# Layer 0 router on four token tiles at once in 32-column parts of TensorE, and an attention end written out without steps

## The chip, the cores and the metric

The kernel runs on one core of one Trainium2 chip. The metric is the device time of one execution, in microseconds (us). Three executions of the kernel before took 3007.15, 3005.03 and 3000.24 us; the median is 3005.03 us. A profiled execution, taken by the hardware profiler, is shown beside them.

Names of engines in the profile: PE is TensorE (PEld its weight loads), DVE is VectorE, ACT is ScalarE, POOL is GpSimd, SP is SyncE, which here only issues DMAs.

## The reference, cut to what matters

Two layers are computed on x, which has 2 x 2048 tokens of 512 numbers (4096 tokens, 32 tiles of 128). Each layer is a cross attention over 154 context rows and a feed-forward part with 8 experts. The change touches only the end of the first attention and the scores by which tokens are given to experts:

```
x = x + xattn(layernorm(x), ctx, w_q, w_k, w_v, w_o)      # 16 heads of 32
xf = layernorm(x).reshape(-1, 512)
scores = softmax(xf @ router_w + router_b, axis=-1)       # 8 experts
G, idx = top_k(scores.T, 1024)                            # each expert picks 1024 tokens
toks = xf[idx]                                            # gathered rows
...
```

All of it is float32.

## The kernel before, in words

**Tiles and steps.** A tile is 128 tokens (`NT` = 32 tiles), a block is four tiles (`TPB` = 4, `NB` = 8 blocks). The first attention runs as a software pipeline: `step(G)` is called for G = 0 to 37 (`for G in range(LAST + 10)`, with `LAST` = 28). One step works on many tiles at once, each at another stage: the scores and exponentials of block-and-head-group G (`scores_of`, `exp_of`, four tiles each), the transposed probabilities of G - 1 (`probs_t`), the product with the values of G - 2 (`values`), the output projection of tile G - 5 (`project`), its residual (`residual`, tile G - 6), the normalised row of tile G - 10 (`norm_x1`, on GpSimd), its transpose (`transpose_x1`, tile G - 11) and the router product of the same tile (`router`). Every fourth step ends with `logits` and `router_scores` of one block.

**What sets the order.** In this stage PE, DVE, ACT and POOL run exactly in the order in which the lines are written; only the order of the DMAs on SP's queue is chosen by the framework's scheduler. An instruction that waits holds up all that stands behind it on its engine.

**Two buffers matter.** The scores live in one PSUM tile `sc` with one buffer, so `scores_of(G, 3)` cannot start on PE before `exp_of(G, 2)` has read the tile of `scores_of(G, 2)`; between the two stand DVE's minimum (L289) and subtraction (L290) and ACT's two exponentials (L301). Nearly all else that PE writes (`ps_q`, `pt`, `pp`, `ps_l`, `ps_o`, `pl`) shares three PSUM buffers with the tag `gen`.

**The router before.** `router(u)` multiplies the router's weights, 128 rows of 8 columns, four times (`KC` = 4 parts of the 512 features) with one transposed tile of 128 tokens. A float32 product takes two passes, so it is 8 instructions on PE (L376). ACT copies the 8 x 128 result to `lT` (L377). When four tiles are there, `logits` turns them back with four small transposes (L384) and DVE and ACT make the softmax; `router_scores` writes the scores into the last 8 columns of each normalised row and sends the row to DRAM (`xs`, L403), 260 KB a tile.

**The end before.** After the loop come the last tiles' norms, transposes and routers. What follows is the choice of 1024 tokens per expert: a search over 30 bits in which DVE and PE take turns (L591 to L595). Its buffers (`sco`, `iota_i`, `same` and others) lie where rows and other tiles of the attention lay, so POOL's first instruction there (L533) and DVE's copy of the scores (L574) wait for the last row store to have landed.

Of the kernel before, what the change touches and what calls it, by code (L numbers as in the profile page):

```python
# [10 lines left out]
F32 = mybir.dt.float32  # L11
# [4 lines left out]
ALU = mybir.AluOpType  # L16
# [18 lines left out]
E = 8  # L35
# [20 lines left out]
def two_layers(ctx: ExitStack, tc: tile.TileContext, a, out):  # L56
# [51 lines left out]
    def transpose_tile(src, dstT, t, psum, tag, bufs=2):  # L108

        pt = psum.tile([P, KC, P], F32, tag=tag, name="pt", bufs=bufs)  # L110
        for k in range(KC):
            nc.tensor.transpose(pt[:, k, :], src[:, ts(k, P)], ident)  # L112
        nc.scalar.copy(dstT[:, :, ts(t, P)], pt)  # L113
# [9 lines left out]
    with (  # L123
# [4 lines left out]
    ):  # L128
        wq = wa.tile([P, KC, D], F32, name="wq")
        wo = wa.tile([P, KC, D], F32, name="wo")  # L130
        rw = wa.tile([P, KC, E], F32, name="rw")
        kT = wa.tile([P, B, KC, TKV], F32, name="kT")
        vblk = wa.tile([P, B, KC, 4, 2, HD], F32, name="vblk")
        scale = HD**-0.5
# [23 lines left out]
        def roots(m):  # L158
            mv, rstd = roots_of(m)
            j = slice(0 if 0 <= m - 2 < NB else 1, 2 if m + 3 < NB else 1)  # L160
            nc.scalar.activation(rstd[:, j], mv[:, j, :, 1], AF.Sqrt, bias=eps_t)
            nc.vector.reciprocal(rstd[:, j], rstd[:, j])
# [29 lines left out]
        with tc.tile_pool(name="wk", bufs=1) as wkv:  # L192
            ctxT = wkv.tile([P, KC, B * TKV], F32, name="ctxT")
            nc.sync.dma_start(ctxT, a["ctxT"].rearrange("(k p) n -> p k n", p=P))
            wk = wkv.tile([P, KC, D], F32, name="wk")
            wv = wkv.tile([P, KC, D], F32, name="wv")
            for w, n in ((wk, "w_kT"), (wv, "w_vT"), (wq, "w_qT"), (wo, "w_oT"), (rw, "router_w")):
                nc.sync.dma_start(w, a[n].rearrange("(k p) n -> p k n", p=P))

            for v in range(TPB):  # L200
                stats(xt[v], -3, 1, v)
            roots(-3)
            for v in range(TPB):
# [28 lines left out]
            for b in range(B):  # L232
                cper = wkv.tile([P, KC, 4, TKV], F32, tag="cper", name="cper")
                for hh in range(4):
                    nc.gpsimd.tensor_copy(cper[:, :, hh, :], ctxT[:, :, ts(b, TKV)])
                for i in range(GC):
                    n = P if i < GC - 1 else GL
                    heads = sorted({i * P // TKV, (i * P + n - 1) // TKV})
                    h0, nh = heads[0], len(heads)
                    ps = pa.tile([P, KC, nh * HD], F32, tag="gen", name="ps_v", bufs=3)  # L240
                    for k in range(KC):
                        nc.tensor.matmul(
                            ps[:n],
                            cper[:, k].rearrange("p h n -> p (h n)")[:, i * P : i * P + n],
                            wv[:, k, :].rearrange("p (c d) -> p c d", c=KC)[:, :, h0 * HD : (h0 + nh) * HD],
                            start=k == 0,
                            stop=k == KC - 1,
                        )
                    for j in range(nh):
                        nc.vector.tensor_scalar_mul(  # L250
                            vblk[:n, b, :, h0 + j, i - h0 - j, :],
                            ps[:n, :, j * HD : (j + 1) * HD],
                            mask[:n, i, h0 + j : h0 + j + 1],
                        )
                    if b == 0 and i > 0:
                        transpose_x(TPB + i - 1)
                    if b == 0 and i < TPB:
                        norm_x(TPB + i)
                        load_x(2 * TPB + i)
                        ps_q = queries(0, i)  # L260
                        nc.scalar.copy(qT[0][:, i, :], ps_q)
                    if b == 1 and i < TPB:
                        stats(xt[2 * TPB + i], -1, 1, i)
            roots(-1)
            for i in range(TPB):
                load_x(3 * TPB + i)
                if i < TPB - 1:
                    stats(xt[3 * TPB + i], 0, 1, i)
            norm_x(2 * TPB)

        with tc.tile_pool(name="sa", bufs=2) as sa:
            prob, pTs, oT, x1t, row, x1T, lT, pend = {}, {}, {}, {}, {}, {}, {}, {}

            def tile_of(u):
                return 0 <= u < NT
# [84 lines left out]

            def norm_x1(u, eng=nc.vector):
                blk, i = divmod(u, TPB)
                row[u] = sa.tile([P, ROW], F32, tag="row", name="row", bufs=8)
                norm(row[u][:, 0:D], x1t.pop(u), blk + 2, 0, i, eng)

            def transpose_x1(u):
                x1T[u] = sa.tile([P, KC, P], F32, tag="x1T", name="x1T", bufs=4)
                transpose_tile(row[u][:, 0:D], x1T[u], 0, pa, "gen", 3)

            def router(u):  # L370
                blk, i = divmod(u, TPB)
                if i == 0:
                    lT[blk] = sa.tile([E, TPB, P], F32, tag="lT", name="lT")
                ps = pa.tile([E, P], F32, tag="gen", name="ps_l", bufs=3)
                for k in range(KC):
                    nc.tensor.matmul(ps, rw[:, k, :], x1T[u][:, k, :], start=k == 0, stop=k == KC - 1)  # L376
                nc.scalar.copy(lT[blk][:, i, :], ps)  # L377

            SL = [P, TPB, E]

            def logits(blk):
                pl = pa.tile(SL, F32, tag="gen", name="pl", bufs=3)
                for t in range(TPB):
                    nc.tensor.transpose(pl[:, t, :], lT[blk][:, t, :], ident[0:E, 0:E])  # L384
                lg = sa.tile(SL, F32, tag="lg", name="lg")
                lm = sa.tile([P, TPB, 1], F32, tag="lm", name="lm")
                nc.vector.tensor_tensor(lg, pl, rb_bc.unsqueeze(1).to_broadcast(SL), ALU.add)
                nc.vector.tensor_reduce(lm, lg, AX.X, ALU.max)
                nc.vector.tensor_tensor(lg, lg, lm.to_broadcast(SL), ALU.subtract)
                nc.scalar.activation(lg, lg, AF.Exp)  # L390
                lT[blk] = (lg, lm)

            def router_scores(blk):
# [6 lines left out]
                for t in range(TPB):  # L400
                    u = blk * TPB + t
                    nc.vector.tensor_copy(row[u][:, D:ROW], scores[:, :, u])
                    nc.sync.dma_start(xs[u * P : (u + 1) * P, :], row.pop(u))  # L403

            LAST = NT - TPB

            def step(G):
                m, i4 = divmod(G, TPB)
# [14 lines left out]
                    residual(G - 6, pend.pop("o"))  # L423
                if tile_of(G + TPB):
                    pend["q"] = queries(m + 1, i4)
                if tile_of(G - 11) and G - 11 < LAST:
                    transpose_x1(G - 11)
                if tile_of(G + 9):
                    norm_x(G + 9, nc.gpsimd)
# [22 lines left out]
                    probs_t(G - 1, 3)  # L452
                if tile_of(G + 8):
                    transpose_x(G + 8)
                if tile_of(G - 10) and G - 10 < LAST:
                    norm_x1(G - 10, nc.gpsimd)
                if tile_of(G - 11) and G - 11 < LAST:
                    router(G - 11)
                if on:
                    scores_of(G, 3)  # L460
                if before:
# [9 lines left out]
                    logits((G - 15) // TPB)  # L471
                    router_scores((G - 15) // TPB)

            for G in range(LAST + 10):
                step(G)
            roots(NB + 1)
            transpose_x1(LAST - 1)
            router(LAST - 1)
            for u in range(LAST, NT):
                norm_x1(u)  # L480
                transpose_x1(u)
            logits(NB - 2)
            router_scores(NB - 2)
            for u in range(LAST, NT):
                router(u)
            logits(NB - 1)
            router_scores(NB - 1)

# [1201 lines left out]
```

## Time and profile before

| What | Value |
|---|---|
| median of three runs | 3005.03 us |
| profiled execution, its own time | 3016.07 us |
| its span in the profile | 3014.4 us |
| granted TensorE clock, mean over the span | 0.966 |
| first attention | about 15 to 628 us of the span |
| end of attention to the first gather of rows | 628 to 711 us |
| everything behind | 711 to 3014 us |
| `ps_l<-x1T,rw` (L376), 256 instructions | 32.8 us of PE busy, 273 ns of one |
| `lT<-ps_l` (L377), 32 copies | 7.9 us of ACT, 250 ns of one |
| `pl<-ident,lT` (L384), 32 transposes | 3.4 us of PE, 208 ns of one |
| `x1T<-pt` (L113), 32 copies | 18.4 us of ACT, 585 ns of one |
| `row<-x,mv,rstd` (L166) on POOL, 28 | 58.0 us, 2072 ns of one |
| `row<-x,mv,rstd` (L166) on DVE, 4 | 540 ns of one |

A group's busy time counts overlapped instructions once, so busy time divided by the count is less than the mean of one: the ends of pipelined products are modelled. To price a group of products on PE, the start of the next group is the better mark. The profiled execution is 11 us (0.37%) above the median.

### The profile page before, as it was taken

How to read it: one execution, taken by the hardware profiler on the slowest of the kernel's cores; microseconds unless marked ns; L12 is line 12 of the kernel's file. 1: busy time of each engine (PE TensorE's matmuls, PEld its weight loads, DVE VectorE, ACT ScalarE, POOL GpSimd, SP SyncE). 2: the span in 40 equal slices, each digit the busy share in tenths (PEclk: the TensorE clock that was granted, in tenths of full speed). 3: DMA queues.
4: the chain of work that ended last, by engine and by line, in shares of the span. 5: the costliest groups of instructions: out<-in, count | busy, mean ns of one | idle time of the engine just before them, and what ended most of it. 6: DMA issues, size and time to landing. Idle time of an engine off the chain costs nothing. (4 is left out here: it accounts for less than half of the span.)

```text
span 3014.4 us, 38792 instructions
## 1 busy us (share of the span) xinstructions
PE 2778.1 (92%) x14262; PEld 2133.2 (71%) x14262; DVE 1547.0 (51%) x2933; ACT 880.1 (29%) x1854; POOL 1216.7 (40%) x986
## 2 busy tenths in 40 slices
PE   7889998867999999999999999999995888889995
PEld 4444554445888888888888888888885655567773
DVE  4677776544545435444454355443532555544355
ACT  2555554411122112212122112211220555432331
POOL 1445544403344424343334333432431555465552
PEclk9899999878999999999999999999998999899998
DMA  4011111161122231231222312312113642143387
GB/s 160 18 36 46 47 61 47 53 219 38 25 77 84 44 111 25 78 86 27 67 81 70 88 22 78 88 29 85 56 15 80 220 81 64 47 92 129 133 315 282
DMA packets 127083, 256.47 MB, mean 85 GB/s; under 512 B 16508, under 2 KB 22668, under 8 KB 126742
## 3 DMA queue, kind: packets, MB, share of 16 engines
q1 hardware_dynamic: 93232, 170.79, 16.9%
q0 software_dynamic: 29056, 74.81, 10.8%
q10 hardware_dynamic: 4608, 8.39, 0.7%
q8 instruction: 115, 1.88, 0.3%
q14 instruction: 72, 0.59, 0.1%
HBM read 176.09 MB, written 77.85 MB: 84 GB/s over the span
## 5 line engine op out<-in xcount | busy, mean ns | idle before, releaser
L831 ACT ACTIVATE H<-H,b_sb 128x256 f32<-128x256 f32 (+1 forms) x384 | 198.9, 571 | 563.0 <-DVE H L882 287.0
L928 POOL TENSOR_TENSOR eo<-eo,b_bc 128x512 f32<-128x512 f32 x64 | 96.4, 1506 | 647.4 <-DVE eo L974 585.4
L709 PE MATMUL prod<-w2q,H 128*128 128x256 f32 x1536 | 346.9, 379 | 0.0
L709 PEld LDWEIGHTS prod<-w2q,H 128*128 128x128 f32 x1536 | 289.5, 190 | 38.1
L312 POOL TENSOR_TENSOR pr<-pr,sm 128x616 f32<-128x616 f32 x128 | 155.2, 1213 | 275.5 <-DVE sm L311 249.7
L709 PE MATMUL prod<-xsum,sw 128*128 128x256 f32 x1024 | 245.4, 380 | 0.7 <-DVE xsum L792 0.7
L709 PE MATMUL prod<-xgT,w1q 128*128 128x256 f32 x1024 | 243.2, 380 | 0.0
L709 PE MATMUL prod<-xgT,sw 128*128 128x256 f32 x1024 | 243.1, 380 | 0.0
L709 PE MATMUL prod<-tw,hs 128*128 128x256 f32 x1024 | 234.5, 380 | 0.0
L817 POOL TENSOR_TENSOR sw<-w1q 128x512 f32<-128x512 f32 x128 | 189.6, 1481 | 84.3 <-PE prod L709 84.0
L709 PEld LDWEIGHTS prod<-xgT,w1q 128*128 128x128 f32 x1024 | 195.5, 191 | 26.8
L709 PEld LDWEIGHTS prod<-tw,hs 128*128 128x128 f32 x1024 | 192.8, 190 | 27.8 <-PE prod L709 2.5
L709 PEld LDWEIGHTS prod<-xsum,sw 128*128 128x128 f32 x1024 | 193.3, 190 | 26.7 <-POOL sw L817 1.0
L709 PEld LDWEIGHTS prod<-xgT,sw 128*128 128x128 f32 x1024 | 193.4, 190 | 25.7
L113 ACT COPY xgT<-pt 128x512 f32<-128x512 f32 x64 | 37.5, 585 | 431.7 <-PE pt L112 431.7
L900 POOL DMA_INDIRECT xacc<-eo,idx x64 | 100.6, 1572 | 153.0 <-DMA xacc<-eo,idx 92.1
L1513 PE MATMUL ph<-xgT,wc 128*128 128x128 f32 x1248 | 152.6, 275 | 7.4 <-DVE wc L1503 6.0
L289 DVE TENSOR_REDUCE mx<-sc 128x4 f32<-128x616 f32 x128 | 101.8, 795 | 105.5 <-PE sc L285 103.5
L1513 PEld LDWEIGHTS ph<-xgT,wc 128*128 128x128 f32 x1248 | 145.6, 192 | 9.0 <-issue 5.3
L1528 PE MATMUL po<-wall,h1r 128*128 x312 | 146.7, 593 | 1.7 <-issue 1.7
L1536 DVE TENSOR_TENSOR y<-po,wall 128x512 f32<-128x512 f32 x78 | 53.9, 691 | 144.1 <-PE po L1528 134.1
L1485 POOL DMA_INDIRECT xg<-xn,xrow x78 | 84.1, 1079 | 106.6 <-PE pt L1120 100.6
(296 smaller groups left out, 5156.9 us busy)
## 6 DMA issues: line engine op xcount, KB each, us to landing
w1q<-in_w SPq DMA_DIRECT2D x32, 1024.0 KB
w2q<-in_w SPq DMA_DIRECT2D x32, 1024.0 KB
y<-ys SPq DMA_DIRECT2D x40, 256.0 KB
xs<-row SPq DMA_DIRECT2D x32, 260.0 KB
x_sb<-in_x SPq DMA_DIRECT2D x32, 256.0 KB
x<-in_x SPq DMA_DIRECT2D x32, 256.0 KB
xacc<-x SPq DMA_DIRECT2D x32, 256.0 KB
x<-xacc SPq DMA_DIRECT2D x32, 256.0 KB
```

The costliest lines, as they stand in the source:

```text
L113: nc.scalar.copy(dstT[:, :, ts(t, P)], pt)
L289: nc.vector.tensor_reduce(mx, sc[:, :, 0:TKV], AX.X, ALU.min)
L312: nc.gpsimd.tensor_tensor(pr, pr, sm.to_broadcast([P, 4, TKV]), ALU.mult)
L709: nc.tensor.matmul(ps[:, g, :], w, m, start=i == 0, stop=i == len(terms) - 1)
L817: nc.gpsimd.tensor_tensor(o, l, m, ALU.add if i == 0 else ALU.subtract)
L831: nc.scalar.activation(dst, src, AF.Relu, bias=b1_sb[:, e, f : f + 1])
L900: nc.gpsimd.indirect_dma_start(out=xacc[:, :], out_offset=bass.IndirectOffsetOnAxis(ap=idx[:, e, col : col + 1], axis=0), in_=eo, in_offse ...
L928: nc.gpsimd.tensor_tensor(eo, eo, b2_bc, ALU.add)
L1485: nc.gpsimd.indirect_dma_start(out=xg[r], out_offset=None, in_=G_.xn[:, :], in_offset=bass.IndirectOffsetOnAxis(ap=G_.xrow[:, i : i + 1], ...
L1513: nc.tensor.matmul(ph[:, c, :], wc[:, k * HE + c * P : k * HE + (c + 1) * P], x_[:, k, :], start=k == 0, stop=k == KC - 1,)
L1528: nc.tensor.matmul(po_[r], h[:, c, :], wflat[:, bass.ds(at + (W2_AT + c * D), D)], start=c == 0, stop=c == HE // P - 1)
L1536: nc.vector.tensor_tensor(y, po_.pop(r), wflat[:, bass.ds(at + B2_AT, D)], ALU.add)
```

## The change

1. `rw` becomes 32 columns wide (`HD` = 32), is set to zero on DVE, and its first 8 columns are loaded.
2. `x1T` holds a whole block; `router(blk)` runs once per block and issues, for each of the four parts of the features, four products, one per tile, each into its own 32 partitions of one PSUM tile. A product is 128 rows by 32 columns, so the four tiles go to four column parts of TensorE, 32 instructions per block (two passes of 16). It stands in the fourth step of a block, where block (G - 15) / 4 is routed, instead of a tile in every step.
3. ACT copies one 128 x 128 `lT` per block, and `logits` turns it back with one transpose.
4. `row` has 12 buffers instead of 8.
5. The steps end with G = 32. What was in steps 33 to 37 and behind the loop is written out: the last four projections stand with only transposes and routers between them; blocks 5, 6 and 7 get their `logits` and `router_scores` at the very end (before, block 5 had them in step 35); the rows of tiles 26 and 27 are normalised on DVE, not POOL; the copy of the last attention output is on ACT, not DVE.

Instruction by instruction, everything behind the attention stands in the same order on PE, DVE, ACT and POOL. On SP one thing moves: the load of the first quarter of expert 0's weights (`w1q`, 1024 KB) stood behind the last eight row stores; in the changed build it stands ahead of the last twelve, and waits there for the last router product. The second quarter comes directly behind those twelve.

```diff
-        rw = wa.tile([P, KC, E], F32, name="rw")
+
+        rw = wa.tile([P, KC, HD], F32, name="rw")
+        nc.vector.memset(rw, 0.0)
...
-            for w, n in ((wk, "w_kT"), (wv, "w_vT"), (wq, "w_qT"), (wo, "w_oT"), (rw, "router_w")):
+            for w, n in ((wk, "w_kT"), (wv, "w_vT"), (wq, "w_qT"), (wo, "w_oT"), (rw[:, :, 0:E], "router_w")):
...
-                row[u] = sa.tile([P, ROW], F32, tag="row", name="row", bufs=8)
+                row[u] = sa.tile([P, ROW], F32, tag="row", name="row", bufs=12)
...
             def transpose_x1(u):
-                x1T[u] = sa.tile([P, KC, P], F32, tag="x1T", name="x1T", bufs=4)
-                transpose_tile(row[u][:, 0:D], x1T[u], 0, pa, "gen", 3)
-
-            def router(u):
                 blk, i = divmod(u, TPB)
                 if i == 0:
-                    lT[blk] = sa.tile([E, TPB, P], F32, tag="lT", name="lT")
-                ps = pa.tile([E, P], F32, tag="gen", name="ps_l", bufs=3)
+                    x1T[blk] = sa.tile([P, KC, TB], F32, tag="x1T", name="x1T")
+                transpose_tile(row[u][:, 0:D], x1T[blk], i, pa, "gen", 3)
+
+            def router(blk):
+
+                ps = pa.tile([P, P], F32, tag="gen", name="ps_l", bufs=3)
+                x_ = x1T.pop(blk)
                 for k in range(KC):
-                    nc.tensor.matmul(ps, rw[:, k, :], x1T[u][:, k, :], start=k == 0, stop=k == KC - 1)
-                nc.scalar.copy(lT[blk][:, i, :], ps)
+                    for t in range(TPB):
+                        nc.tensor.matmul(
+                            ps[t * HD : (t + 1) * HD, :], rw[:, k, :], x_[:, k, ts(t, P)], start=k == 0, stop=k == KC - 1
+                        )
+                lT[blk] = sa.tile([P, P], F32, tag="lT", name="lT")
+                nc.scalar.copy(lT[blk], ps)
...
             def logits(blk):
-                pl = pa.tile(SL, F32, tag="gen", name="pl", bufs=3)
-                for t in range(TPB):
-                    nc.tensor.transpose(pl[:, t, :], lT[blk][:, t, :], ident[0:E, 0:E])
+                pl = pa.tile([P, TPB, HD], F32, tag="gen", name="pl", bufs=3)
+                nc.tensor.transpose(pl.rearrange("p t e -> p (t e)"), lT[blk], ident)
...
-                if tile_of(G - 11) and G - 11 < LAST:
+                if tile_of(G - 11):
                     transpose_x1(G - 11)
...
-                if tile_of(G - 10) and G - 10 < LAST:
+                if tile_of(G - 10):
                     norm_x1(G - 10, nc.gpsimd)
-                if tile_of(G - 11) and G - 11 < LAST:
-                    router(G - 11)
+                if i4 == 3 and tile_of(G - 15):
+                    router((G - 15) // TPB)
...
-            for G in range(LAST + 10):
+
+
+            for G in range(NT + 1):
                 step(G)
-            roots(NB + 1)
-            transpose_x1(LAST - 1)
-            router(LAST - 1)
-            for u in range(LAST, NT):
+            L5, L6, L7 = NB - 3, NB - 2, NB - 1
+            u5, u6, u7 = L5 * TPB, L6 * TPB, L7 * TPB
+            load_x1(NT - 2)
+            load_x1(NT - 1)
+            av = values(NT - 1)
+            residual(u6 + 3, pend.pop("o"))
+            nc.scalar.copy(*av)
+            roots(L6 + 2)
+            transpose_x1(u5 + 2)
+            norm_x1(u5 + 3, nc.gpsimd)
+            norm_x1(u6, nc.gpsimd)
+            norm_x1(u6 + 1, nc.gpsimd)
+            pend["o"] = project(u7)
+            residual(u7, pend.pop("o"))
+            norm_x1(u6 + 2)
+            transpose_x1(u5 + 3)
+            pend["o"] = project(u7 + 1)
+            residual(u7 + 1, pend.pop("o"))
+            norm_x1(u6 + 3)
+            router(L5)
+            pend["o"] = project(u7 + 2)
+            residual(u7 + 2, pend.pop("o"))
+            transpose_x1(u6)
+            transpose_x1(u6 + 1)
+            pend["o"] = project(u7 + 3)
+            residual(u7 + 3, pend.pop("o"))
+            roots(L7 + 2)
+            transpose_x1(u6 + 2)
+            transpose_x1(u6 + 3)
+            router(L6)
+            for u in range(u7, NT):
                 norm_x1(u)
                 transpose_x1(u)
-            logits(NB - 2)
-            router_scores(NB - 2)
-            for u in range(LAST, NT):
-                router(u)
-            logits(NB - 1)
-            router_scores(NB - 1)
+            for blk in (L5, L6):
+                logits(blk)
+            router(L7)
+            for blk in (L5, L6):
+                router_scores(blk)
+            logits(L7)
+            router_scores(L7)
```

More of the change, by code (lines that the diff above doesn't have):

```diff
@@ L379, in two_layers @@
             SL = [P, TPB, E]
             def logits(blk):
-                pl = pa.tile(SL, F32, tag="gen", name="pl", bufs=3)
-                for t in range(TPB):
-                    nc.tensor.transpose(pl[:, t, :], lT[blk][:, t, :], ident[0:E, 0:E])
+                pl = pa.tile([P, TPB, HD], F32, tag="gen", name="pl", bufs=3)
+                nc.tensor.transpose(pl.rearrange("p t e -> p (t e)"), lT[blk], ident)
                 lg = sa.tile(SL, F32, tag="lg", name="lg")
                 lm = sa.tile([P, TPB, 1], F32, tag="lm", name="lm")
-                nc.vector.tensor_tensor(lg, pl, rb_bc.unsqueeze(1).to_broadcast(SL), ALU.add)
+                nc.vector.tensor_tensor(lg, pl[:, :, 0:E], rb_bc.unsqueeze(1).to_broadcast(SL), ALU.add)
@@ L403, in router_scores @@
                     nc.sync.dma_start(xs[u * P : (u + 1) * P, :], row.pop(u))
-            LAST = NT - TPB
             def step(G):
```

## The prediction

> **What bounds the kernel now.** I read the page first, then the busy times in windows to see which engine is dense in the first attention, then PE's timeline step by step, then the queues of SP and POOL at the stage's end.
>
> ```profile
> PE 2778.1 (92%) x14262; PEld 2133.2 (71%) x14262; DVE 1547.0 (51%) x2933; ACT 880.1 (29%) x1854; POOL 1216.7 (40%) x986
> ...
> 220.00:300.00 80.00, 75.63 (x488) 40.19 (x484) 59.16 (x115) 43.13 (x103) 44.65 (x30) 1.00 0.16 47
> 300.00:380.00 80.00, 76.81 (x500) 40.49 (x492) 58.41 (x127) 42.11 (x105) 41.66 (x29) 1.00 0.16 53
> ```
>
> Columns of the windows: stretch, then busy time of PE, PEld, DVE, ACT, POOL, granted clock, DMA share, GB/s. PE is busy 95% of the steps, DVE 74%: a product removed may shorten a step, unless something else was to wait for anyway. That is read from two steps of PE's timeline (start, time, what; in brackets PE's idle time and its releaser): step 8 has no router yet, step 11 has one.
>
> ```profile
> 188.77 0.54 PE L285 MATMUL sc<-kT,qT 32*128 32x154 f32 x8
> 189.25 1.09 PE L318 MATMUL pp<-ident,pr 128*128 128x128 f32 x8
> 190.18 0.60 PE L112 MATMUL pt<-ident,xn 128*128 128x128 f32 x4
> 191.54 0.54 PE L285 MATMUL sc<-kT,qT 32*128 32x154 f32 x8 [0.76 <-ACT pr L301]
> ...
> 236.51 0.54 PE L285 MATMUL sc<-kT,qT 32*128 32x154 f32 x8
> 236.98 1.09 PE L318 MATMUL pp<-ident,pr 128*128 128x128 f32 x8
> 237.91 0.60 PE L112 MATMUL pt<-ident,xn 128*128 128x128 f32 x4
> 238.44 1.04 PE L376 MATMUL ps_l<-x1T,rw 128*8 128x128 f32 x8
> 239.41 0.54 PE L285 MATMUL sc<-kT,qT 32*128 32x154 f32 x8
> ```
>
> The router takes 239.41 - 238.44 = 0.97 us of PE, but without it the fourth scores group waits 0.76 us for the exponentials: from third to fourth group it is 2.77 us without the router and 2.90 with it. To the projection it is 192.50 - 188.77 = 3.73 against 240.56 - 236.51 = 4.05 us, since without a router the `pp` group is also spared its wait for a PSUM buffer. **A router in a step is worth 0.32 us, not 0.97.** From step 24 on, where no `xn` tile is transposed, the router itself is followed by a 0.23 us wait and the same distance is 3.72 us: there it is worth nothing.
>
> At the stage's end the bound changes:
>
> ```profile
> 624.66 4.96 SPq L403 DMA_DIRECT2D xs<-row  x8
> 629.72 0.49 SPq L502 DMA_DIRECT2D w1q<-in_w  x1
> 632.39 0.38 SPq L514 DMA_DIRECT2D ctxT<-in_ctxT  x1
> ...
> 632.65 0.23 POOL L533 IOTA iota_i<- 128x128 int32 x1 [30.10 <-DMA xs<-row]
> ...
> 626.00:628.00 2.00, 0.27 (x2) 0.30 (x2) 1.53 (x10) 0.23 (x1) 0.00 (x0) 1.00 1.03 389
> ```
>
> The last scores are copied into rows by 628.0, but POOL and the search go on only when the last row store has landed, 632.4. The DMA engines are then full, at 389 GB/s. So what counts is when the last row lands.
>
> **The parts of the change.**
>
> *The router product, R per block.* It is 8 rounds of four instructions. If the four column parts work side by side, a round lasts one instruction's stream. The nearest row is the value product, the same shape (128 rows, 32 columns, four parts in turn, 128*32 in the trace):
>
> ```profile
> 589.32 1.93 PE L333 MATMUL av<-pT,vblk 128*32 128x512 f32 x16
> 591.06 1.04 PE L376 MATMUL ps_l<-x1T,rw 128*8 128x128 f32 x8
> ```
>
> Its 16 instructions of 512 columns take 591.06 - 589.32 = 1.74 us, 109 ns each; a full-width one (`ps_o`, 8 in 3.53 us) takes 441. That is fourfold overlap. For 128 columns the stream is 110 ns (L376), so R = 8 x 0.11 + 0.1 for the change of groups = 1.0 us. A rule speaks against it: the Trainium skill, "TensorE: Matmul & The Clock Gate", Part 2 ("Back-to-back issue gap"), says that without hardware decoding the sequencer spends about 62 ns on each matmul, which binds once the array's work is shorter. Overlapped, the array's work is 28 ns an instruction: 32 x 62 ns is R = 2.0 us. The scores groups (8 in about 0.48 us, 60 ns each) would fit it, but their figure holds the change of groups too; the eight list products (L752) of 0.36 us show at most 45 ns each. I take R = 1.05 by the `av` row, with 1.0 and 2.0 as ends.
>
> *Steps 11 to 32.* Ten of the thirteen steps from 11 to 23 lose their router (all but 15, 19, 23): 10 x 0.32 = 3.2 us gained. Steps 15, 19, 23 have R instead of 0.97: 3 x 0.08 = 0.25 lost (3.1 at R = 2.0). Steps 27 and 31 have 0.23 us to spare: nothing (1.6 lost at R = 2.0). Steps 24 to 30 gain nothing. `logits` before costs 0.23 us a block between projection and queries (four transposes); one costs about 0.13: 5 x 0.1 = 0.5 gained. Step 32 has no scores to wait for and loses a full 0.97.
>
> *The end.* In the profile's own clock, step 32's projection ends at 588.8 before, 587.8 after. PE then has the values (1.75), four projections (4 x 3.53), transposes of 22 to 25 (4 x 0.53) and router 5 (1.05), nearly without waits: the second root (L161) comes at 592 and POOL's two rows at 596.5, used from 602.5 on. The last projection ends at about 607.0 against 613.6 before: one router product stands between instead of four, and the waits for `x1T` copies (0.67 + 0.68 + 0.88) and one `logits` are gone. From there the chain of before repeats: residual, statistics, root, reciprocal, four DVE norms, to about 611.4. Transposes 26, 27 stand ready, but their ACT copies stand behind the root, so router 6 waits about 2 us and ends near 611.4; then come four transposes with copies to 614.1, a table load of 1.28 us and the exponentials. DVE now has two blocks' scores to write first, 2 x 1.08 us, but all under 618. The last rows are copied at about 619.9 against 628.0.
>
> *What is late next: the queue.* Before, eight stores (2.13 MB) ended the stage; now twelve (3.19 MB) and, ahead of them, `w1q` (1.05 MB), released by router 7 at about 615.3. First bytes come 0.85 us after an issue (624.66 to about 625.5): 616.1. 4.24 MB at 380 GB/s are 11.2 us: the last row lands at **627.3**. Twelve issues of 0.47 us (four in 1.87) would allow 625.1, so the transfer decides. Behind the twelve, the second `w1q` goes before `ctxT` and `wk`; these land about 1 us later after the last row than before, but the first `ps_k` comes 15 us after it and the biases 13.5 us after, so nothing waits. 632.4 - 627.3 is 5.1 us, of which step 32's 0.97 is part.
>
> *At nothing:* the memset of `rw` (DVE, some 0.1 us, under the first weight loads), fewer `lT` copies (ACT is 29% busy), the norms of 26 and 27 on DVE, which idles 2.6 to 4.4 us between residuals, and twelve `row` buffers. Without that cover the two norms would cost 1.1 us.
>
> *The clock.* The same page, Part 1, says that after an idle window of some 3.4 us TensorE runs at half clock until busy again. In the trace a 1.40 us wait at 412.6 is followed by a value product of 3.1 us instead of 1.86, yet before the last router of the steps a 1.84 us gap leaves 0.97 us. By the row router 6 costs nothing more after its 2 us wait; by the rule's worst case it and the four transposes lose 3 us. I take nothing and keep 3 us for the range.
>
> **Sum.** 3.2 - 0.25 + 0.5 + 5.1 = 8.5 us. From the profiled 3016.07 that gives 3007.5; from the median, 3005.03, **2996.5**. The 11 us between lie in the execution, not in this stage, so I put the gain on the median: 2997.
>
> **Rivals.**
>
> *The gain of the end goes into the queue (0.26).* For it: in 630 to 632 us the engines are as full but move only 296 GB/s. At 300 GB/s the 4.24 MB take 14.1 us and land at 630.2; with 2.0 us for R or the 3 us of clock, later still. Left are about 3 us: 3002. Against it: that slice mixes stores and loads, and the loads behind run at 383 to 389.
>
> *The four parts don't overlap (0.12), slower.* The place is `router(blk)`, the price 32 x 110 ns + 0.1 = 3.6 us. Steps 15, 19, 23 lose 2.63 each, 27 and 31 lose 2.4 each, less 3.7 gained: 9.0 us lost. In the end each of three routers adds 2.6 to the chain that releases `w1q`, which then goes at 623 and holds the rows behind it: landing at 635.2, 2.8 lost. Sum 11.8: 3017. It decides from R of about 2.2. Against it stands the `av` row.
>
> *The forecast: 0.62.*
>
> **How the numbers follow.** What a measurement of this kernel can tell from no change is about 0.2%, 6 us. The forecast's own spread is the landing (625 to 629) and R, gain 4 to 11, and the runs' own 7 us; most of it, and a little of the first rival, lies below 2999: faster 0.60. Same 0.27: the queue rival and the forecast's low end. Slower 0.13: no overlap. The range runs from 2988 (gain 11, a low run) to 3008 (R = 2.0 with the clock's 3 us and a high run).
>
> **What would show it.** `ps_l` groups of 32 in about 1.0 us; fourth scores groups with a 0.76 us wait in router-free steps and 3.73 us to the projection; step 24 on unchanged; `w1q` issued near 612 (the steps' 3.5 us taken off 615.3), the last landing (POOL's L533) near 624 instead of 632.4, DMA full in between; the search and all behind unchanged in length. It is wrong if `ps_l` takes over 2 us, if the rows land no earlier, or if the stretch behind the search is longer.

## The result and the profile after

The changed kernel takes 2998.19 us (median of 20 runs, 2990.27 to 3008.57); the kernel before, on the same chip, 3003.75 us (20 runs, 3000.24 to 3008.47). The ratio is 0.9982 with a 95% interval of 0.9974 to 0.9989, which is 5.6 us faster (3.3 to 7.8).

The profiled execution spans 2995.4 us against 3014.4. Most of those 19 us are not the change: when the last row of the attention has landed, the gap is 4.5 us, and at the first gather of rows 5.7 us (711.18 before, 705.52 after). The rest comes behind about 2310 us, in a stage that the diff does not touch and whose length differs between executions of one kernel: a second profile of the kernel before spans 2997.8 us, reaches its last scatter of layer 0 within 0.5 us of the first profile, and then needs 685.4 us where the first needed 701.6. At that last scatter the two profiles of before stand at 2312.8 and 2312.4 us and two of the changed kernel at 2307.1 and 2306.9: 5.3 to 5.9 us, as at the first gather. So the readings below stop at the first gather.

**The router and a step without it.** PE's timeline after: step 11, which has no router now, then step 15, which has one.

```profile
236.82 0.54 PE L287 MATMUL sc<-kT,qT 32*128 32x154 f32 x8
237.30 1.09 PE L320 MATMUL pp<-ident,pr 128*128 128x128 f32 x8
238.23 0.60 PE L112 MATMUL pt<-ident,xn 128*128 128x128 f32 x4
239.59 0.55 PE L287 MATMUL sc<-kT,qT 32*128 32x154 f32 x8 [0.76 <-ACT pr L303]
...
240.55 1.88 PE L354 MATMUL ps_o<-wo,oT 128*128 128x512 f32 x4
...
302.89 1.08 PE L380 MATMUL ps_l<-x1T,rw 128*32 128x128 f32 x32
303.90 0.54 PE L287 MATMUL sc<-kT,qT 32*128 32x154 f32 x8
```

The fourth scores group waits 0.76 us for the exponentials, and third group to projection is 240.55 - 236.82 = 3.73 us, as in step 8 before the change. The 32 router instructions take 303.90 - 302.89 = 1.01 us. The end of step 23 (its `logits` transpose), counted from the start of step 11, is at 209.66 us; before, 212.87.

**The end of the attention.** PE's timeline from the last projection on:

```profile
600.77 3.70 PE L354 MATMUL ps_o<-wo,oT 128*128 128x512 f32 x8
604.31 1.04 PE L112 MATMUL pt<-ident,row 128*128 128x128 f32 x8
605.32 0.41 PE L380 MATMUL ps_l<-x1T,rw 128*32 128x128 f32 x4
607.06 1.55 PE L380 MATMUL ps_l<-x1T,rw 128*32 128x128 f32 x28 [1.33 <-ACT x1T L113]
608.54 2.05 PE L112 MATMUL pt<-ident,row 128*128 128x128 f32 x16
...
611.17 1.29 PE L380 MATMUL ps_l<-x1T,rw 128*32 128x128 f32 x32
...
616.66 0.49 PE L607 MATMUL pt_s<-ident,scores 128*128 128x128 f32 x2 [3.13 <-DVE scores L403]
630.38 0.56 PE L613 MATMUL pc<-cnt,same 128*128 128x1 f32 x2 [13.23 <-DVE io_t L568]
```

The same three places before the change:

```profile
610.07 3.70 PE L352 MATMUL ps_o<-wo,oT 128*128 128x512 f32 x8
...
627.73 0.48 PE L573 MATMUL pt_s<-ident,scores 128*128 128x128 f32 x2 [1.77 <-DVE scores L397]
634.91 0.56 PE L579 MATMUL pc<-cnt,same 128*128 128x1 f32 x2 [6.70 <-DVE io_t L534]
```

The last projection starts 9.3 us earlier, and the finished scores reach the search's transposes (`pt_s`) 11.1 us earlier. But the search's first count (`pc`) starts only 4.5 us earlier, after 13.23 us of idleness. SP's queue and then POOL show why:

```profile
612.61 0.38 SPq L536 DMA_DIRECT2D w1q<-in_w  x1
613.79 9.07 SPq L409 DMA_DIRECT2D xs<-row  x12
622.92 0.68 SPq L536 DMA_DIRECT2D w1q<-in_w  x1
627.84 0.38 SPq L548 DMA_DIRECT2D ctxT<-in_ctxT  x1
```

```profile
628.12 0.23 POOL L567 IOTA iota_i<- 128x128 int32 x1 [33.99 <-DMA xs<-row]
```

POOL goes on when the last row has landed, at 628.12. The DMA engines were busy to that moment (windows after; the last column is GB/s, the one before it the DMA share):

```profile
614.00:616.00 2.00, 0.00 (x0) 0.00 (x0) 1.47 (x11) 0.23 (x1) 0.00 (x0) 1.00 0.85 256
616.00:618.00 2.00, 0.49 (x2) 0.31 (x2) 0.84 (x7) 0.00 (x0) 0.00 (x0) 0.75 0.91 275
618.00:620.00 2.00, 0.00 (x0) 0.00 (x0) 0.00 (x0) 0.00 (x0) 0.00 (x0) 0.50 1.04 398
...
626.00:628.00 2.00, 0.00 (x0) 0.00 (x0) 0.00 (x0) 0.00 (x0) 0.00 (x0) 0.50 1.04 384
```

Over the eight windows from 612 to 628 they moved 4.96 MB: one `w1q` of 1.05 MB, twelve rows of 3.19 MB, and, what is left of the sum, some 0.7 MB of the second `w1q`, issued at 622.92 while rows were still on their way. **Of 11.1 us won at the scores, 6.5 were given back in this queue.**

### The profile page after: what moved, and what is told of

It is laid out like the page before. It is cut to its first block, busy times and chain, and to the rows that moved or that the text cites. A ratio compares the mean times of both kernels' runs of the same rounds, so it can differ in the third digit from the quotient of the medians.

```text
span 2995.4 us, 38713 instructions
## 1 busy us (share of the span) xinstructions
PE 2750.0 (92%) x14238; PEld 2114.6 (71%) x14238; DVE 1557.9 (52%) x2935; ACT 874.1 (29%) x1829; POOL 1209.9 (40%) x984
## 5 line engine op out<-in xcount | busy, mean ns | idle before, releaser
L851 POOL TENSOR_TENSOR sw<-w1q,sw 128x512 f32<-128x512 f32 x64 | 91.7, 1433 | 87.2 <-PE prod L743 87.2
```

The costliest lines, as they stand in the source:

```text
L851: nc.gpsimd.tensor_tensor(o, l, m, ALU.add if i == 0 else ALU.subtract)
```

## The experiments

Executions start their steps up to 3 us apart, so times are counted from the start of step 11 (first scores group: 228.61 us before, 228.93 after). "Scores" is the start of `pt_s`, "landed" POOL's first search instruction, "gather" the first gather of rows. Each ratio is to executions of the kernel before in the same series (their medians: 3003.75 us for the result; 3021.69, 3006.64 and 3002.93 us in the three series of experiments). Even so one kernel's scores repeat only to about 2 us (395.2 and 393.3 in the two profiles of end_only): a step's 16 value products take some 3.5 us instead of 1.85 where the clock is low, and which steps that meets varies.

| kernel | scores | landed | gather | ratio to before (95%) |
|---|---|---|---|---|
| before | 399.1 | 404.0 | 482.6 | 1 |
| before_again | 399.0 | 403.9 | 482.5 | 1.0005 (0.9995 to 1.0015) |
| changed | 387.7 | 399.2 | 476.6 | 0.9982 (0.9974 to 0.9989) |
| after_again | 386.5 | 397.8 | 475.9 | 0.9979 (0.9969 to 0.9988) |
| hold_weights | 386.7 | 394.2 | 470.3 | 0.9955 (0.9941 to 0.9968) |
| hold_again | 386.9 | 394.3 | 470.5 | 0.9958 (0.9945 to 0.9970) |
| early_block5 | 387.8 | 397.5 | 476.1 | 0.9976 (0.9966 to 0.9986) |
| hold_and_early | 387.8 | 393.3 | 469.9 | 0.9950 (0.9935 to 0.9965) |
| tile_outer | 390.8 | 403.3 | 480.3 | 0.9995 (0.9985 to 1.0004) |
| steps_only | 385.2 | 394.9 | 473.6 | 0.9971 (0.9961 to 0.9982) |
| end_only | 395.2 | 402.3 | 482.2 | 0.9982 (0.9975 to 0.9989) |
| end_only_again | 393.3 | 400.2 | 480.1 | 0.9991 (0.9982 to 1.0000) |
| steps_hold | 387.4 | 393.0 | 467.6 | 0.9942 (0.9929 to 0.9956) |

The theory to begin with: the queue decides the landing, and the weights in it are what gives the gain back. The rival: rows and their issues take that long in any case.

### The weights taken out of the way (hold_weights)

The changed kernel, with expert 0's weight loads ordered behind the small bias loads, so that no weights stand among the rows:

```diff
-            nc.sync.dma_start(bv_bc, a["bv"].partition_broadcast(P))
+            bv_ld = nc.sync.dma_start(bv_bc, a["bv"].partition_broadcast(P))
             for q in range(4):
-                load_w1(0, q)
+                ld = load_w1(0, q)
+                tc.add_manual_dep(ld.ins, bv_ld.ins.name, ORDER_DEP, reason="behind the row stores")
...
```

(The same two lines follow for `load_w2`.)

> The changed kernel with one thing altered: expert 0's weight loads (w1q and w2q) stand on SP's queue behind the load of bv, so none of them is ahead of the last twelve row stores or among them. Theory 1, the transfer decides: in the changed kernel 4.96 MB moved from 612 us until the last row landed at 627.84 us, of which 1.05 MB was the first w1q and about 0.7 MB the second; without them 3.19 MB from 614.6 us at 380 GB/s end at 623.0 us, so POOL's first instruction of the search starts at about 623.3 instead of 628.12, and the time falls by about 4.8 us against the changed kernel, to about 2993 us (ratio to before about 0.9966). Theory 2, SP's issuing decides (twelve stores in 9.07 us): the last issue ends at 622.9 as before and the landing is 2.7 us later, 625.6; 2.2 us gained. Theory 3, the weights were wanted early: POOL starts earlier, but the first expert's sums start no earlier, and nothing is gained.

In the profile's own clock POOL starts at 622.75, where the transfer theory said 623.3 and the issuing theory 625.6. Landed is 3.6 to 5.0 us earlier than in the two profiles of the changed kernel, at unchanged scores, and the ratio falls to 0.9955, further than the 0.9966 expected. The repetition beside the changed kernel itself:

> The changed kernel with expert 0's weight loads ordered behind the small bias loads, beside the changed kernel on the same chip. Theory 1: 4 to 6 us below the changed kernel again (ratio to before 0.995 to 0.9965 where the changed kernel has 0.998), last row 5 to 6 us after the scores instead of 11.5. Rival (the earlier run of it was a fast one): no more than 2 us below the changed kernel.

> The changed kernel itself, as the yardstick on the same chip for the two halves and for the kernel that holds the weights back. All theories: ratio to before 0.997 to 0.999, routers in about 1.0 us, POOL's first search instruction 11 us after the scores.

In the same series the changed kernel has the ratio 0.9979: the two ratios differ by 0.0021, 6.3 us (the medians, 2992.19 and 3000.49 us, by 8.3). SP's queue and the windows of hold_again:

```profile
612.62 7.20 SPq L409 DMA_DIRECT2D xs<-row  x12
622.63 0.38 SPq L548 DMA_DIRECT2D ctxT<-in_ctxT  x1
```

```profile
614.00:616.00 2.00, 0.51 (x2) 0.32 (x2) 1.28 (x9) 0.23 (x1) 0.00 (x0) 0.50 1.03 388
616.00:618.00 2.00, 0.16 (x1) 0.00 (x0) 0.00 (x0) 0.00 (x0) 0.00 (x0) 0.50 1.03 388
618.00:620.00 2.00, 0.00 (x0) 0.00 (x0) 0.00 (x0) 0.00 (x0) 0.00 (x0) 0.50 1.02 384
```

Stores alone run at 384 to 388 GB/s from the start, where the queue that began with `w1q` ran at 256 and 275. From scores to landing it is 7.4 us (5 to 6 were expected) instead of 11.4: the weights' share is 4 us. The twelve rows keep the other 2.5 us (before, with eight, the distance is 4.9). The gain at the gather is larger than at the landing, 5.4 to 6.3 us, because the stretch from landing to gather also got shorter (76.1 to 76.2 us instead of 77.4 to 78.1).

That second part is not the queue's. The edit did more than its lines say: with the weights held back, the scheduler also placed the context's key and value products (`ps_k` to `ps_v`) two counts of the search earlier in PE's order. The same holds for hold_and_early and steps_hold; the other kernels have PE's order of before. All this lies behind the landing, so the 4 us there stand; what it is worth at the gather is told at the end of this document.

### Four rows out early (early_block5, hold_and_early)

Block 5's `logits` and `router_scores` go between the last projections, so that four rows leave some 10 us earlier; first alone, then with the weights held back.

```diff
             residual(u7 + 2, pend.pop("o"))
+            logits(L5)
             transpose_x1(u6)
             transpose_x1(u6 + 1)
+            router_scores(L5)
...
-            for blk in (L5, L6):
-                logits(blk)
+            logits(L6)
             router(L7)
-            for blk in (L5, L6):
-                router_scores(blk)
+            router_scores(L6)
```

> The changed kernel with the logits and scores of block 5 put before the last projection, where DVE and ACT idle, and those of block 6 alone before the last router; the first w1q stays ahead of the last stores, which are eight instead of twelve. Theory 1, the transfer decides: 1.06 MB of rows are gone from the end; 4.96 - 1.06 = 3.9 MB at the same mean rate of some 330 GB/s from 613 us end at about 624.5 us, POOL starts at about 624.8, 3.3 us earlier than in the changed kernel; about 2995 us. Theory 2, issuing decides: eight issues of 0.76 us from about 614 us end by 620, landing at 623. Theory 3, the two table loads that come back on ACT (exponential and root, 1.28 us each) stand on the chain: the last scores come 1.3 us later or more and half of the gain is lost.

> Both edits together: eight row stores at the end and no weight load ahead of them. Theory 1, the transfer decides: the last scores are copied at about 616 us, the eight stores (2.13 MB) are issued by 618.3 and land at about 621, as in the kernel before where the landing was 2.7 us behind the last issue; POOL starts at about 621.3, 6.8 us before the changed kernel; about 2991 us, ratio to before about 0.996. Theory 2, the gain of an earlier search is taken back behind it (weights late, or the search longer): POOL starts near 621 but the time stays within 2 us of the changed kernel's 2998.

Scores to landing falls to 9.7 us with the weights still there and to 5.5 us without them. Each of the two causes is seen alone and together: weights about 4 us, the four extra rows about 1.7 to 1.9. In landing early_block5 is 0.3 to 1.7 us ahead of the changed kernel, less than the 3.3 us expected, and hold_and_early about 1 us ahead of hold_weights (4.5 to 5.9 us ahead of the changed kernel; 6.8 were expected); the ratios do not tell either pair apart.

### The order inside the router (tile_outer)

```diff
-                for k in range(KC):
-                    for t in range(TPB):
+                for t in range(TPB):
+                    for k in range(KC):
```

> The changed kernel with the two loops of the router exchanged: all four feature parts of one token tile, then the next tile, so that eight instructions in a row go to the same column part of TensorE. Same products, same count. Theory 1, the parts overlap only because neighbours in the order lie in different parts: a ps_l group of 32 takes about 32 x 110 ns + 0.1 = 3.6 us instead of 1.01; steps 15, 19, 23 are 2.6 us longer each, 27 and 31 about 2.4, the three routers of the end 2.6 each; about 12 us in the end of the steps and 8 in the tail, together the time about 12 to 20 us above the changed kernel, 3010 to 3018. Theory 2, the four parts have queues of their own and the order inside the group does not matter: ps_l stays near 1.0 us and nothing changes.

PE's timeline of tile_outer:

```profile
304.67 2.46 PE L380 MATMUL ps_l<-x1T,rw 128*32 128x128 f32 x32
307.06 0.55 PE L287 MATMUL sc<-kT,qT 32*128 32x154 f32 x8
```

The same 32 instructions, eight to one column part and then eight to the next, take 2.39 us instead of 1.01. It is not a full loss of overlap either, which the prediction had priced at 3.6 us. With 2.39 us the change is worth nothing that can be measured (0.9995, interval 0.9985 to 1.0004), although the end's order is that of the changed kernel: that fits the prediction's break-even of about 2.2 us.

### The two halves (steps_only, end_only)

steps_only has the new router everywhere but the old end; end_only has the new end but the router tile by tile, in 8 columns.

```diff
...
+            LAST = NT - TPB
+            for G in range(LAST + 10):
+                step(G)
+            roots(NB + 1)
+            transpose_x1(LAST - 1)
+            router(NB - 2)
+            for u in range(LAST, NT):
+                norm_x1(u)
+                transpose_x1(u)
+            logits(NB - 2)
+            router_scores(NB - 2)
+            router(NB - 1)
+            logits(NB - 1)
+            router_scores(NB - 1)
...
```

(Cut: the written-out lines go, and transposes and norms of the last four tiles leave the steps.)

> One part of the change alone: the router in four column parts (one product of 32 instructions a block, in the steps and in the end), with the end of the attention as it was before (remaining tiles in the order of the old loop, eight rows stored at the very end instead of twelve). Theory 1 (the end's shorter chain is partly given back in the DMA queue, where w1q goes ahead of the last rows and a second w1q is mixed in among them): step 23 ends 3.2 us earlier than before, counted from step 11, as in the changed kernel; the chain of the end loses single-tile routers and their x1T waits and is some 8 to 10 us earlier at the scores; but the queue holds only 8 rows (2.1 MB instead of 3.2) behind w1q, so the last row lands no later than in the changed kernel: POOL's first search instruction at 624 to 628 in the frame in which the changed kernel has 628.1, ratio to before 0.997 to 0.999. Rival (the rewritten end is what brings the gain, the steps only 3 us): the last row at 629 or later, ratio 0.999 to 1.000.

Here the old end reaches the scores as early as the written-out end (8 to 10 us ahead of before were expected, 13.9 came). The 385.2 flatters it, since fewer of its steps met the low clock: on the same PE work of the steps the steps_hold kernel below was 2.3 us later at its first projection behind step 32, so 387.5 is the fairer figure, beside 386.5 and 387.7. With that correction it lands at 397.2, also no later than the changed kernel's 397.8 and 399.2. **With the new router in place, the end written without steps brings no time.** What the queue of steps_only does is as in the theory:

```profile
610.05 0.38 SPq L508 DMA_DIRECT2D w1q<-in_w  x1
611.24 6.28 SPq L409 DMA_DIRECT2D xs<-row  x8
617.57 0.63 SPq L508 DMA_DIRECT2D w1q<-in_w  x1
622.57 0.38 SPq L520 DMA_DIRECT2D ctxT<-in_ctxT  x1
```

Two weight loads stand around eight rows here too, and scores to landing is 9.7 us, not 4.9.

For the other half, which routes tile by tile:

```diff
...
-                    for t in range(TPB):
-                        nc.tensor.matmul(
-                            ps[t * HD : (t + 1) * HD, :], rw[:, k, :], x_[:, k, ts(t, P)], start=k == 0, stop=k == KC - 1
-                        )
+                    nc.tensor.matmul(ps, rw[:, k, 0:E], x1T[blk][:, k, ts(i, P)], start=k == 0, stop=k == KC - 1)
...
```

> The other part alone: the end of the attention written out as in the change, with the router tile by tile in 8 columns, as before (in the steps for the first five blocks; in the end four tiles in turn, 3.7 to 3.9 us a block where the changed kernel takes 1.0 to 1.3). Here w1q happens to stand behind the row stores on SP's queue, as before the change. Theory 1: the steps stand as before (3.2 us later than in the changed kernel at the end of step 23); in the end three routers cost up to 2.7 us more each, so the scores come some 10 us later than in the changed kernel, at about the time of before; but with no weights among the rows the last row lands about 5 us after the scores (before: 4.9) and not 11.5 (changed kernel): about the time of before, ratio 0.999 to 1.001. Rival (the queue is full with twelve rows in any case, weights or not): the distance from scores to landing stays at 10 us or more, landing 5 us later than before, ratio 1.001 to 1.003.

> The same kernel as end_only, whose comparison with before (0.9982) and whose trace (rows land 1.7 us earlier, first gather 0.3 us earlier than before, counted from step 11) did not agree. By the trace: first gather within 2.5 us of before, ratio 0.999 to 1.000. By the comparison: ratio 0.998 again, with the time found in the last stage behind the first layer's experts.

> The kernel before the change, once more as a kernel of its own, to see how far the comparison and the landmarks of one profile repeat. Ratio 0.9995 to 1.0005; counted from step 11 the last row lands at 404 us and the first gather starts at 482 to 483 us, as in its first profile; only the stages behind the first layer's experts vary by several us.

The two profiles of this kernel have the scores 3.9 and 5.8 us ahead of before (nothing was expected), about half or less of the changed kernel's 11.4 to 12.6. In its queue the twelve rows go first (issued from 620.31 on in end_only) and `w1q` behind them (627.62). From the scores 7.1 and 6.9 us pass to the landing: not the 5 us expected (twelve rows take longer than eight), and not the 10 us of the rival. It lands 1.7 and 3.8 us ahead and gathers 0.3 and 2.4 us ahead. The first ratio, 0.9982, had promised more; the second says 0.9991, and their intervals overlap from 0.9982 to 0.9989. The landmarks of before and before_again agree to 0.2 us and the ratio to 0.0005, but the two profiles of end_only differ by 2 us. So the new end with the old router is worth something between 0.3 us (the first gather) and 5.4 us (the first ratio); a firmer figure was not obtained.

### Both lessons together (steps_hold)

steps_only, with the weight loads held back by the same lines as in hold_weights.

> The router in four column parts with the old end of the attention (as in steps_only), and expert 0's weight loads ordered behind the small bias loads (as in hold_again). Theory (the written-out end brings no time, the queue took what the router had gained): with eight stores and no weights among them the last row lands about 5 us after the scores, as before the change (4.9), not 9.7 as in steps_only; that is 4 to 5 us earlier than steps_only and 2 to 4 us earlier than hold_again, each counted from step 11. Ratio to before 0.9935 to 0.996, at or below hold_again's 0.9958. Rival (the written-out end does bring time once the queue is free, so the best is the changed kernel with the weights held back): landing no earlier than in hold_again, ratio 0.996 or more.

PE's timeline and SP's queue of steps_hold:

```profile
600.87 3.70 PE L354 MATMUL ps_o<-wo,oT 128*128 128x512 f32 x8
...
617.38 0.48 PE L581 MATMUL pt_s<-ident,scores 128*128 128x128 f32 x2 [2.26 <-DVE scores L403]
625.17 0.56 PE L587 MATMUL pc<-cnt,same 128*128 128x1 f32 x2 [7.32 <-DVE io_t L542]
```

```profile
602.43 1.79 SPq L409 DMA_DIRECT2D xs<-row  x4
604.32 1.74 SPq L360 DMA_DIRECT2D xacc<-x  x2
615.53 4.45 SPq L409 DMA_DIRECT2D xs<-row  x8
622.64 0.38 SPq L520 DMA_DIRECT2D ctxT<-in_ctxT  x1
```

Block 5's four rows are gone at 602.43, in the old loop's step 35; eight are left, no weights among them, and PE's idle wait ahead of the first count is 7.32 us where the changed kernel's is 13.23. It is the fastest kernel tried: 2986.39 us against 3002.93, ratio 0.9942 (0.9929 to 0.9956), 17 us. The landing is 1.2 to 1.3 us ahead of the two profiles with the written-out end and held weights, less than the 2 to 4 expected; the gather is 2.7 to 2.9 us ahead, 1.5 us of it in the counts of the search, which met a higher clock (end of this document). The intervals of the ratios overlap, so it is shown that this version beats the changed kernel, and not that the written-out end costs time once the weights are held back.

## Why the prediction was right, and where its sum was off

Forecast: 2997 us, faster. Measured: 2998.19 us, 0.9982, inside the range. The gain summed to 8.5 us, and 5.6 (3.3 to 7.8) came: the direction and most of the mechanism were right, the size was not. That the level missed by only 1.2 us is in part luck, since the three runs of before from which it was counted have a median 1.3 us above that of the twenty.

- **R, the router of a block:** taken as 1.05 us by the row of the value products, measured 1.01. The 62 ns an instruction (2.0 us) that the Trainium skill, "TensorE: Matmul & The Clock Gate", Part 2 ("Back-to-back issue gap"), gives for TensorE without hardware decoding did not bind these groups: 32 instructions in 1.01 us are 32 ns each.
- **Steps 11 to 32:** 3.2 gained, 0.25 lost and 0.3 for three `logits` make 3.25 to the end of step 23; measured 3.21. The 0.76 us wait and the 3.73 us came out to the hundredth. That the sums agree is luck all the same: two errors cancel, as told behind this list. From step 24 on nothing more came, except 0.24 us by step 27's `logits` (503.14 - 228.93 against 506.27 - 228.61).
- **The end's chain:** last rows copied at 619.9 in the clock of before, 616.4 with the steps' 3.5 us taken off; the last copy ended at 616.95. `w1q` "near 612": 612.61. The prediction credited that to fewer router products and fewer `x1T` waits. The runs confirm the first part and change the second: most of these waits go in the old end too (steps_only), so it is the one router per block that removes them, not the order written out.
- **The step that failed is the queue.** "4.24 MB at 380 GB/s are 11.2 us", landing at 623.8 with the steps' 3.5 us taken off; it landed at 627.84 by SP's queue (POOL starts 0.28 us later). The term is mis-sized in three places: the release came 0.8 us later than assumed; the first four microseconds ran at 256 and 275 GB/s instead of 380, which costs about 4 x (380 - 266) / 380 = 1.2 us; and the second `w1q`, named as standing behind the twelve rows and priced at nothing for them, moved some 0.7 MB among them, 1.9 us at 380. Together 3.9 of 4.0 us. That weights cost the rows their time is shown by hold_weights and hold_again (4 us); how it divides into these three is argued from the windows.
- **The rivals.** "The gain of the end goes into the queue" named the right place: at the landing 4.9 to 6.2 us are left of 11.4 to 12.6, and the forecast had 8.5. It did not decide the outcome, since its 3 us were too little. Its mechanism, 300 GB/s all through, was wrong: the rate is low only at the start, and the load is larger. "The four parts don't overlap" did not happen, but tile_outer shows how near it was: the other order of two loops gives 2.39 us and takes the whole gain.
- **The clock:** router 6 waited 1.33 us (2 forecast), and the windows from 604 to 612 us show a granted clock of 1.00: the row was right, and the worst case of 3 us was not met. Its last 28 instructions still took 608.54 - 607.06 = 1.48 us, but not for their own length: two start at once, the other 26 from 607.55 on, released by ACT's next `x1T` copy, and those take 0.99 us. That second wait stood at nothing in the sum.
- **"The search and all behind unchanged in length"** held for the order of instructions, but not for the length to the microsecond: 77.4 and 78.1 us from landing to gather against 78.5 and 78.6 before.

**Why the steps' sum agrees.** The first error: a router-free step is 0.43 us shorter from projection to projection (15.15 us against 15.58), not 0.32. The prediction stopped at the projection, but the first scores group behind it also comes 0.10 us sooner (3.53 us, 240.55 to 244.08, against 3.63 before, 240.56 to 244.19).

The second: in the changed profile the value products of steps 14, 18 and 22 met a low clock, before the change only those of step 22. Step 14 of the changed kernel, then of steps_only:

```profile
281.61 0.77 PE L320 MATMUL pp<-ident,pr 128*128 128x128 f32 x5 [1.40 <-POOL pr L314]
282.31 3.53 PE L335 MATMUL av<-pT,vblk 128*32 128x512 f32 x16
...
280.64 0.77 PE L320 MATMUL pp<-ident,pr 128*128 128x128 f32 x5 [1.41 <-POOL pr L314]
281.33 1.93 PE L335 MATMUL av<-pT,vblk 128*32 128x512 f32 x16
```

The wait ahead is the same, but the granted clock over the products is 0.53 in the one and 1.00 in the other, and the step lasts 18.7 us from projection to projection against 17.9. steps_only has one such slow step between 11 and 23, as before has, and ends step 23 4.87 us ahead of it (208.00 against 212.87). That is the size of the term at equal clock; two more slow steps, at 0.8 us each, took 1.6 us of it in the changed profile.

Of the nine profiles with a router per block, seven have three slow steps there and two have one; the four with the router tile by tile have one or none. Why is open. In the changed profile the clock falls at 282.48, 347.34 and 412.19 us, each time for 3.413 us; the distance, 64.85 us, is 19 times that, and a block with a slow step lasts 65.0 us (before the change 65.7). So the same step may be met block after block; this was not tested.

## What to carry to other kernels

When a change frees an engine ahead of a transfer that ends the stage, count every transfer of that queue up to the landing, also what stands behind the awaited one: a load issued right behind the last stores moves bytes among them. A prefetch that has 80 us to spare belongs behind the stores that the next stage waits for. Try each half of a double change with the other taken out: here the router brought the time, the rewritten end none that was measurable beside it, and one ordering of the weight loads, which neither half contained, brought about as much again (another 0.0021 of the ratio in one series, where the change had brought 0.0021).

Two cautions stand beside that. An edit that only orders loads can let the scheduler reorder the engines' instructions as well, so compare their order before a gain is put down to the loads. And a sum that meets its measured value to the hundredth can still hide two errors of opposite sign: look at a second kernel in which one of them is absent.

## What was not expected of the hardware

**The order of column parts.** The same 32 products on four column parts take 1.01 us when the parts take turns and 2.39 us when each part gets its eight in a row. With no overlap at 110 ns each it would be 3.6 us, so the second order still overlaps in part; what limits it was not tried.

**A stretch that is not all search, and runs with the clock.** From landing to gather it took 74.7 to 80.0 us. The way to the first count is 2.3 us in every profile. From the last count to the gather it is 29.0 us in the nine profiles with PE's order of before, and 27.3 in the four with the weights held back. PE's last count, the context's value products and DVE's next step, in the changed kernel and then in hold_again:

```profile
676.54 0.37 PE L613 MATMUL pc<-cnt,same 128*128 128x1 f32 x2
682.25 10.46 PE L699 MATMUL ps_v<-wv,ctxT 128*77 128x512 f32 x24
697.91 0.43 DVE L762 TENSOR_TENSOR ohhi<-hi,io 128x256 bf16<-128x256 bf16 x1 [4.47 <-DMA vp_d<-vp]
...
671.77 0.38 PE L615 MATMUL pc<-cnt,same 128*128 128x1 f32 x2
677.56 8.75 PE L701 MATMUL ps_v<-wv,ctxT 128*77 128x512 f32 x20
691.50 0.42 DVE L764 TENSOR_TENSOR ohhi<-hi,io 128x256 bf16<-128x256 bf16 x1 [4.48 <-DMA vp_d<-vp]
```

DVE goes on towards the gather only when the store of the context's values (`vp_d`) has landed. With PE's other order four fewer of their products stand behind the search, and that is the 1.6 us. So the context's products are on the path to the gather, and this part of the gain of the held weights comes from an order on PE.

In between lie the counts themselves, and they follow the clock. With PE's order of before, the first to the last count take 45.7 us at a mean granted clock of 0.74 (tile_outer), 47.3 at 0.72 (before) and 48.7 at 0.68 (end_only); with the other order 45.1 at 0.78 (steps_hold) and 46.6 at 0.76 (hold_again), against 46.2 and 46.8 in the two profiles of the changed kernel. Counts with nothing else on PE start 1.55 us apart at half clock and 1.35 us at the full one. The clock rises some 4 to 8 us after the first key products (`ps_k`) have begun to fill PE; that link is read from the traces and was not tested by itself.
